# The rows of an MLP norm transposed by VectorE and placed by DMAs, in place of TensorE's transposes

## The chip, the cores and the metric

The kernel runs on one core of a Trainium2 chip. The metric is the time of one execution on the device, in microseconds (us). The core has five engines that run side by side, each with its own queue of instructions in a fixed order: TensorE (PE in the profile; its weight loads are PEld), VectorE (DVE), ScalarE (ACT), GpSimd (POOL) and SyncE (SP), which issues nearly all of this kernel's DMAs.

## The reference

Input rows `x` (4 batches, 1024 tokens, 512 features, float32) first pass a graph-attention layer, then a transformer block with six modulation vectors made from a condition. Only the last part of the block matters here, the MLP with its layer norm:

```python
x = x + g_msa * _attention(_modulate(_layernorm(x), sh_msa, sc_msa), W_qkv, W_out, b_out)
x = x + g_mlp * _ff(_modulate(_layernorm(x), sh_mlp, sc_mlp), W1, b1, W2, b2)

def _modulate(x, shift, scale):
    return x * (1.0 + scale) + shift
def _ff(x, W1, b1, W2, b2):
    return jax.nn.gelu(x @ W1 + b1, approximate=False) @ W2 + b2
```

The hidden width of the MLP is 2048. Everything is float32.

## The kernel before, in words

The 4096 rows are 32 tiles of 128 rows (`NTA`), and the MLP stage, the last of three, takes them in eight blocks of four tiles (`VB = 4`, the loop over `k` from L1603). The rows after attention lie in DRAM as `x2d[0..31]`.

For each block the normalised rows are needed with the features along the partitions: the tile `hT[1, 0]`, 128 partitions by 4 feature chunks by 512 rows. There is one such tile, and every block uses it. It is the moving operand of the up projection.

Both projections are done by a scheme with seven products in place of eight block products (`seven`, L520, and `with_four`, L564, which makes it seven steps: a, c, b, a2, b2, d, b3). A step is a group of matmuls into one PSUM bank and then some work on it by ScalarE or VectorE: after a, ScalarE copies the bank (L555); after c, `keep_c` copies it to SBUF on ScalarE (L544); after b, `start_d` on VectorE writes bank d (L547), which the product d adds to; after b2, `last` on VectorE reads bank b (L551), which the product b3 then adds to. The scheme needs sums of input pieces: `mlp_rows` (L630) makes them from `hT[1, 0]` on GpSimd with four operations (L512), into places 0 to 2 of the tile `tx["mlp"]`, the third of them in place in `hT`. The first is needed by product c, the second by b, the third by b2, the last by b3. Places 3 and 4 of the same tile hold the gate and the bias of the current batch, spread over all partitions; place 5 is not used.

One block `k` goes so:

- `norm_load(1, k + 1)` loads the four row tiles of the next block from `x2d` into `xl` (four buffers, L412).
- The up projection: four groups `p`, each with seven steps into the banks `up_banks` ("mau" to "mdu" in the profile), a Gelu on ScalarE (L661) and four sums on VectorE (`up_sums`, L504 to L507). In group 2, `norm_rows` normalises the next block's rows in place on VectorE (L425).
- The down projection: seven steps into `dn_banks` ("mad" to "mdd"). After each step's matmuls `dn_done` (L1653) multiplies by the gate and adds to the row tiles `rows2` on VectorE (L1656, L1661), and the finished halves are stored on SP (L1664).
- After the first step of the down projection `between()` (L1637) is called, once a block. It transposes the next block's rows with `norm_T` (L433): for each of the four feature chunks, four TensorE transposes (L443) into a bank of the up projection (`new_bank`, L1592, alternates between two), then one operation that applies scale and shift and writes `hT[1, 0]`, on ScalarE (L448) or VectorE (L450), in turn; in block 0 all four on ScalarE. Then it loads gate and bias for a new batch (every second block), loads the block's rows once more as `rows2` (they take the four `xl` buffers, so each load waits until the transposes have read them), makes the sums by `mlp_rows`, and adds the bias to each `rows2` on GpSimd (L1651).

In block 0 VectorE also makes sums of the weights `w2` just before the down projection (L1626). The rows of the very first block are transposed earlier, inside the attention stage, by the same `norm_T`.

No planner orders this stage: every engine's instructions stand in the order in which this code emits them. An engine whose next instruction waits holds all that stands behind it. A tile's buffers are handed on by waiting for the last reader.

Two older places do on other data what the change will do here: in the attention stage `turn` (L1184) transposes 32x32 blocks on VectorE and moves them by DMAs from SBUF to SBUF (`wT<-wd`, L1195); and at the start `spread_values` (L363) moves many pieces of 128 bytes (`vb<-vrd`).

Of the kernel before, what the change touches and what calls it, by code (L numbers as in the profile page):

```python
# [12 lines left out]
F32 = mybir.dt.float32  # L13
I32 = mybir.dt.int32
AF = mybir.ActivationFunctionType
ALU = mybir.AluOpType
# [3 lines left out]
P = 128  # L20
S = 1024
F = 512
FC = F // P
NT = S // P
# [17 lines left out]
def cond_block_kernel(  # L42
# [27 lines left out]
    nc = tc.nc  # L70
# [27 lines left out]
    modT = cst.tile([P, 4 * FC, B], F32, name="modT")  # L98
    SH_A, SC_A, SH_M, SC_M = 0, FC, 2 * FC, 3 * FC
# [20 lines left out]
    def spread(k, b, o):  # L120

        nc.sync.dma_start(o, gated[32 * k + b : 32 * k + b + 1, :].broadcast_to([P, F]))
# [6 lines left out]
    x2d = [tc.dram_tile([P, F], F32, name=f"x2d{i}") for i in range(NTA)]  # L129


    with ExitStack() as gctx:
# [272 lines left out]
        rp = ctx.enter_context(tc.tile_pool(name="rp", bufs=1, side="right", reuse_waits="tile"))  # L405
        qp = ctx.enter_context(tc.tile_pool(name="qp", bufs=1, side="right", reuse_waits="tile"))
        xp = ctx.enter_context(tc.tile_pool(name="xp", bufs=1, side="right", reuse_waits="tile"))
        VB = 4
        xl, hT, wqk, wv, qT, kT, w1g, part = {}, {}, {}, {}, {}, {}, {}, {}
# [23 lines left out]
        def norm_T(st, k, c, bank, on_act=True):  # L433

            sh, sc = NORM[st][4:]
            b = k * VB // NT
            if st == 1 and k > 0:
                hT[st, k] = hT[st, 0]
            elif c == 0:
                hT[st, k] = rp.tile([P, FC, VB * P], F32, name="hT", tag="hT", bufs=2)  # L440
            pt = bank("ptn")
            for n in range(VB):
                nc.tensor.transpose(  # L443
                    pt[:, n * P : (n + 1) * P], xl[st, k * VB + n][:, c * P : (c + 1) * P], ident
                )
            scale, shift = modT[:, sc + c, b : b + 1], modT[:, sh + c, b : b + 1]
            if on_act:
                nc.scalar.activation(hT[st, k][:, c, :], pt, AF.Identity, scale=scale, bias=shift)  # L448
            else:
                nc.vector.tensor_scalar(hT[st, k][:, c, :], pt, scale, shift, ALU.mult, ALU.add)  # L450

        def load_w(held, key, tag, src, cols):

# [136 lines left out]
        ex, tx = {}, {}  # L590
# [350 lines left out]
    with ExitStack() as actx:  # L941
# [298 lines left out]
        for b in range(B):  # L1240
# [22 lines left out]
            for gp in range(NP):  # L1263
                g, p = divmod(gp, 2)
# [284 lines left out]
    with ExitStack() as mctx:  # L1549
        mp = mctx.enter_context(tc.tile_pool(name="mp", bufs=1, reuse_waits="tile"))  # L1550
        hs[2] = mp.tile([P, NT, HB], F32, name="hs2")
        hs[3] = mp.tile([P, NT, HB], F32, name="hs3")
        for i in (6, 7):
            put_w1(i, mp.tile([P, FC, 2, P], F32, name=f"w1_{i}"))
        for i in range(4, MC // 2):
            mlp_weights(nc.vector, i, lambda: mp.tile([P, 3 * HB], F32, name="ex", tag="ex", bufs=4))
        emit(NS + 4, NS + 24)
        octx.close()
        pctx.close()
        mp2 = mctx.enter_context(tc.tile_pool(name="mp2", bufs=1, reuse_waits="tile"))  # L1560
        ps = mctx.enter_context(tc.tile_pool(name="ps3", bufs=1, space=PSUM))
        w2s = [mp2.tile([P, 4, F], F32, name=f"w2_{k}") for k in range(4)]
        for k in (0, 2, 1, 3):
            nc.sync.dma_start(w2s[k], w2[k * F : (k + 1) * F, :].rearrange("(c p) f -> p c f", p=P))
        w2x = [mp2.tile([P, 3, 4, HB], F32, name=f"w2x{k}") for k in range(2)]
        for p in range(4):
            hx[p] = mp2.tile([P, 3, 2, HB], F32, name=f"hx{p}")
        up_banks, dn_banks = (
            {n: ps.tile([P, F], F32, name=n + x) for n in ("ma", "mb", "mc", "md")} for x in "ud"
        )  # L1570
        for banks in (up_banks, dn_banks):
            for n in ("mb", "md"):
                nc.tensor.matmul(banks[n], lhsT=ident, rhs=hT[1, 0][:, 0, :], start=True, stop=True)
        gate2, bias2 = (tx["mlp"][:, k, :] for k in (3, 4))

        def dn_lhs(which, t, c):
            p, q = divmod(c, 2)
            rows = slice(t * P, (t + 1) * P)
            at = {4: 0, 5: 1, 2: 2}.get(which)
            if at is not None:  # L1580
                return hx[p][:, at, q, rows]
            return hs[p][:, 2 * {0: 0, 1: 1, 6: 2, 3: 3}[which] + q, rows]

        def dn_rhs(which, t, c):
            k, r = divmod(c, 4)
            at = {4: 0, 5: 1, 3: 2}.get(which)
            if at is not None:
                return w2x[k][:, at, r, :]
            h, f = {0: (0, 0), 1: (1, 0), 2: (1, 1), 6: (0, 1)}[which]
            return w2s[2 * h + k][:, r, f * HB : (f + 1) * HB]  # L1590

        def new_bank(name):  # L1592

            flip.append(0)
            return up_banks[("ma", "mc")[len(flip) % 2]]

        def short():
            return mp2.tile([P, F], F32, name="s", tag="s", bufs=2)

        flip = []  # L1600
        rows2 = {}
        NB2 = NTA // VB
        for k in range(NB2):  # L1603
            b = k * VB // NT
            nxt = k + 1
            if nxt < NB2:
                norm_load(1, nxt)
            for p in range(2 if k == 0 else 0, 4):
                steps = with_four(
                    get=up_banks.get, short=short, lhs=up_lhs(p), rhs=up_rhs, nk=2,  # L1610
                    room=lambda: hidden(p, 1, 1), done=lambda i, j, t: gelu(p, i, j, t),
                )
                for n, f in enumerate(steps):
                    f()
                    if k == 0 and n == (4 if p == 2 else 2):

                        for j in ((0, 1) if p == 2 else (2,)):
                            up_sums(j)
                if k > 0:
                    up_sums(p)  # L1620
                elif p == 3:
                    sums = []
                    for j in range(2):
                        o = [w2x[j][:, n] for n in range(3)]
                        q, r = w2s[j], w2s[2 + j]
                        sums.append(steps_b(nc.vector, o, q[:, :, :HB], q[:, :, HB:], r[:, :, :HB], r[:, :, HB:]))  # L1626
                    for n, two in enumerate(zip(*sums)):
                        for f in two:
                            f()
                        if n == 0:  # L1630
                            up_sums(p)
                if p == 1 and k == 1:
                    rstd(rs2, mv2, nm2, 3 * NT, NTA)
                if p == 2 and nxt < NB2:
                    norm_rows(1, nxt)

            def between():  # L1637
                if nxt < NB2:
                    for c in range(FC):
                        norm_T(1, nxt, c, new_bank, on_act=(k == 0 or c % 2 == 1))  # L1640
                if k * VB % NT == 0:
                    spread(2, b, gate2)
                    spread(3, b, bias2)
                for n in range(VB):
                    i = k * VB + n
                    rows2[n] = rp.tile([P, F], F32, name="x2", tag="xl", bufs=VB)
                    nc.sync.dma_start(rows2[n], x2d[i])
                if nxt < NB2:
                    mlp_rows()
                for n in range(VB):  # L1650
                    nc.gpsimd.tensor_tensor(rows2[n], rows2[n], bias2, ALU.add)  # L1651

            def dn_done(i, j, t):  # L1653
                y = t if (i, j) == (1, 1) else short()
                g = gate2[:, j * HB : (j + 1) * HB].unsqueeze(1).to_broadcast([P, 2, HB])
                nc.vector.tensor_tensor(  # L1656
                    y.rearrange("p (t f) -> p t f", t=2), t.rearrange("p (t f) -> p t f", t=2), g, ALU.mult
                )
                for n in range(2):
                    o = rows2[2 * i + n][:, j * HB : (j + 1) * HB]  # L1660
                    nc.vector.tensor_tensor(o, o, y[:, n * HB : (n + 1) * HB], ALU.add)  # L1661
                    if (i, j) in ((0, 1), (1, 0)):
                        at = k * VB + 2 * i + n
                        nc.sync.dma_start(out[at * P : (at + 1) * P, :], rows2[2 * i + n])  # L1664

            steps = with_four(
                get=dn_banks.get, short=short, lhs=dn_lhs, rhs=dn_rhs, nk=MC // 2, room=None, done=dn_done
            )
            for n, f in enumerate(steps):
                f()  # L1670
                if n == 0:
                    between()


# [48 lines left out]
```

## Time and profile before

| | us |
|---|---|
| median of three runs | 3037.48 |
| lowest and highest of the three | 3035.5 and 3040.55 |
| span of the profiled execution, first to last instruction | 3034.2 |
| TensorE busy in it | 2999.3 (99%) |
| VectorE, ScalarE, GpSimd busy | 1999.6, 1432.0, 1339.4 |
| the MLP's up and down products, from 2262 us on | 772 of the span |
| one block of the MLP stage, start to start | 99.2 |

No time of its own is given for the profiled execution besides its span; the span lies 3.3 us under the median of the three runs and 1.3 us under the lowest.

How the profile is read: "busy" is the time in which an engine worked on something. The forty slices are equal parts of the span (76 us each), and each digit is the busy share in tenths. The chain of waits starts at the last instruction and goes back from each step to what released it. In a row of instructions, `hT<-mcu,modT` means that `hT` is written from `mcu` and `modT`; then come the shapes, the count after x, the busy time and the mean in ns. Rows marked SPq are DMA instructions on SP's queue: their times are those of issuing, not of moving the bytes.

### The profile page before, as it was taken

The page shows a single profiled execution, that of the slowest core. Times are in us where ns is not written, and L with a number is a line of the kernel's source. Part 1 is how long each engine was busy: PE and PEld are TensorE (multiplying, and loading weights), DVE is VectorE, ACT ScalarE, POOL GpSimd, SP SyncE. Part 2 cuts the span into 40 slices and gives each one's busy share as a digit, 9 for nine tenths or more (in the row PEclk, how much of TensorE's full clock was granted, in tenths as well). Part 3 has the DMA queues.
Part 4 walks back from the last instruction along what each step waited for, and adds up shares of the span by engine and source line. Part 5 has one row for each costly group of instructions (what it writes and reads, how often), then busy time and mean ns, then how long its engine had stood idle before and what let it go on. Part 6 is the DMA issues. An engine that isn't in the chain of part 4 may idle for free.

```text
span 3034.2 us, 41780 instructions
## 1 busy us (share of the span) xinstructions
PE 2999.3 (99%) x15317; PEld 1980.2 (65%) x15317; DVE 1999.6 (66%) x2836; ACT 1432.0 (47%) x2368; POOL 1339.4 (44%) x922
## 2 busy tenths in 40 slices
PE   9999999999999999999999999999999999999999
PEld 6666655555555555555555555555568888888888
DVE  3888867777878877878787878877863222222322
ACT  3344456555755565755555755556641221112211
POOL 1444456555656655656655656655721110111010
PEclk9999999999999999999999999999999999999999
DMA  6433357777868777768777868766871010101110
GB/s 201 140 118 121 117 129 180 162 171 179 192 157 210 181 168 179 192 155 211 187 159 180 191 159 205 189 162 164 203 196 63 14 49 28 49 21 35 35 42 15
DMA packets 282695, 417.90 MB, mean 138 GB/s; under 512 B 28968, under 2 KB 101092, under 8 KB 282492
## 3 DMA queue, kind: packets, MB, share of 16 engines
q1 hardware_dynamic: 282256, 415.03, 53.8%
q8 instruction: 123, 2.02, 0.3%
q14 instruction: 80, 0.66, 0.1%
q10 hardware_dynamic: 236, 0.20, 0.0%
HBM read 120.93 MB, written 25.76 MB: 48 GB/s over the span
## 4 chain that ended last, share of the span: by engine, by line
PE 83%; DVE 7%; ACT 3%; POOL 3%; issue 2%; DMA 2%; SPq 1%; POOLq 0%; DVEq 0%; ACTq 0%
PE q L533 19%; PE psc L1156 15%; PE pav L1064 13%; PE pu L1139 6%; PE mbd L533 5%; PE mbu L533 5%; PE mad L533 4%; PE mau L533 3%; PE mcd L533 2%; PE mdd L533 2%; PE mdu L533 2%; PE mcu L533 2%; DVE mx L1167 1%; ACT w L1173 1%; POOL t L742 1%
## 5 line engine op out<-in xcount | busy, mean ns | idle before, releaser
L1182 POOL TENSOR_SCALAR w<-w,sm 128x1024 f32<-128x1024 f32 x256 | 728.6, 2846 | 701.5 <-DVE sm L1178 686.4
L1173 ACT ACTIVATE w<-psc,mx 128x1024 f32<-128x1024 f32 x512 | 570.7, 1115 | 642.6 <-DVE mx L1167 641.6
L1191 DVE STREAM_TRANSPOSE wd<-w 128x1024 f32<-128x1024 f32 x512 | 632.2, 1235 | 109.3 <-ACT w L1180 96.0
L1167 DVE TENSOR_REDUCE mx<-psc 128x1 f32<-128x1024 f32 x512 | 599.2, 1211 | 80.2 <-PE psc L1156 77.0
L1156 PE MATMUL psc<-kT,qT 64*128 64x512 f32 x2048 | 526.9, 615 | 3.1 <-ACT kT L1024 1.4
L1064 PE MATMUL pav<-wT,v 128*64 128x256 f32 x4096 | 482.1, 383 | 1.2 <-DMA wT<-wd 0.6
L1064 PEld LDWEIGHTS pav<-wT,v 128*64 128x64 f32 x4096 | 296.1, 137 | 224.0 <-issue 86.0
L1156 PEld LDWEIGHTS psc<-kT,qT 64*128 64x128 f32 x2048 | 201.6, 186 | 220.5 <-issue 151.2
L1180 ACT ACTIVATE w<-w,sm 128x1024 f32<-128x1024 f32 x256 | 291.0, 1137 | 0.0
L512 POOL TENSOR_TENSOR tx<-hT 128x512 f32<-128x512 f32 x8 | 10.3, 1288 | 596.5 <-ACT hT L448 596.5
L1148 DVE TENSOR_TENSOR xr<-pu,xr 128x512 f32<-128x512 f32 x210 | 143.5, 683 | 78.9 <-PE pu L1139 78.7
L533 PE MATMUL q<-hT,wqk 128*128 128x512 f32 (+1 forms) x396 | 181.2, 581 | 1.0 <-DVE q L547 1.0
L555 ACT COPY mbu<-mau 128x512 f32<-128x512 f32 x30 | 17.1, 570 | 276.5 <-PE mau L533 276.5
L719 PE MATMUL pa<-kp,sfT 128*128 128x320 f32 x512 | 143.5, 433 | 1.4 <-ACT sfT L694 1.4
L533 PEld LDWEIGHTS q<-hT,wqk 128*128 128x128 f32 x396 | 74.7, 190 | 80.9 <-issue 78.2
L533 PE MATMUL q<-tx,ex 128*128 128x512 f32 (+1 forms) x264 | 123.5, 591 | 1.8 <-POOL tx L618 1.3
L719 PEld LDWEIGHTS pa<-kp,sfT 128*128 128x128 f32 x512 | 94.8, 190 | 38.2 <-ACT sfT L694 1.9
L679 PE MATMUL pf<-wx,xT 128*128 128x512 f32 x256 | 116.0, 596 | 0.0
L533 PE MATMUL mad<-w,hs 128*128 128x256 f32 x512 | 113.1, 379 | 0.0
L533 PEld LDWEIGHTS mad<-w,hs 128*128 128x128 f32 x512 | 97.3, 190 | 13.2
L1139 PE MATMUL pu<-wout,oT 128*128 128x256 f32 x360 | 98.4, 396 | 4.2 <-DVE xr L1148 3.7
L1139 PEld LDWEIGHTS pu<-wout,oT 128*128 128x128 f32 x360 | 62.6, 189 | 59.3 <-issue 31.6
(309 smaller groups left out, 4590.7 us busy)
## 6 DMA issues: line engine op xcount, KB each, us to landing
wT<-wd SPq DMA_DIRECT2D x1024, 256.0 KB
wqk<-in_w_qkv SPq DMA_DIRECT2D x64, 256.0 KB
xT<-in_xt SPq DMA_DIRECT2D x32, 256.0 KB
xs<-in_x SPq DMA_DIRECT2D x32, 256.0 KB
x1d<-xs SPq DMA_DIRECT2D x32, 256.0 KB
xl<-x1d SPq DMA_DIRECT2D x32, 256.0 KB
wv<-in_w_qkv SPq DMA_DIRECT2D x32, 256.0 KB
xr<-x1d SPq DMA_DIRECT2D x32, 256.0 KB
```

What stands on the lines that cost most here:

```text
L533: nc.tensor.matmul(t[:, q * width : (q + 1) * width], lhsT=lhs(which, q, k), rhs=rhs(which, q, k), start=(fresh and q == 0 and k == 0), st ...
L679: nc.tensor.matmul(pfs[i], lhsT=xT[i][:, c, :], rhs=wx[:, c, :], start=False, stop=(c == FC - 1), skip_group_check=True,)
L719: nc.tensor.matmul(pas[i][:, n, :HF], lhsT=sfT2[i][:, c, :], rhs=kp[:, b, c, n * HF : (n + 1) * HF], start=False, stop=(c == FC - 1), skip ...
L1064: nc.tensor.matmul(po[j * D : (j + 1) * D, :], lhsT=vt[b, g][:, m, p * P + j * D : p * P + (j + 1) * D], rhs=w[:, j, :, m, :], start=(m == 0),
L1139: nc.tensor.matmul(pu[0][:, q * HB : (q + 1) * HB], lhsT=a[:, q * P : (q + 1) * P], rhs=r, start=(bool(fresh) and q == 0), stop=True, skip ...
L1148: nc.vector.tensor_tensor(o, pu[0].rearrange("p (r f) -> p r f", r=2), o, ALU.add)
L1156: nc.tensor.matmul(sc[j][:, n * F : (n + 1) * F], lhsT=qT[b, gp][q, t * P : (t + 1) * P], rhs=kT[b, gp][q, n * F : (n + 1) * F], start=Tru ...
L1167: nc.vector.tensor_reduce(mx, sc, axis=AX.X, op=ALU.max, negate=True)
L1173: nc.scalar.activation(w, sc, AF.Exp, bias=mx, accum_out=sm)
L1180: nc.scalar.mul(w, w, sm)
L1182: nc.gpsimd.tensor_scalar(w, w, sm, None, ALU.mult)
L1191: nc.vector.transpose(wd[j][:, :, at, :], wn.pop((b, gp, t, j)).rearrange("p (m k) -> p m k", k=U))
```

## The change

For the MLP stage's second to eighth block the transposes leave TensorE. `norm_turn` transposes one tile of 128 rows on VectorE: one instruction that transposes each 32x32 block where it lies, from `xl` into place 5 of `tx["mlp"]`. What is then still in the wrong place is moved by sixteen DMAs: one for each pair of a group `u` of 32 rows (now a group of 32 partitions) and a group `v` of 32 features. Each moves 32 partitions by four feature chunks by 32 values, 16 KB in pieces of 128 bytes, into `hT[1, 0]`. All are issued by SP. `norm_mod` then applies scale and shift in place in `hT[1, 0]` on ScalarE, one instruction for each feature chunk.

`between` is now called after each of the seven steps of the down projection. After each of the first four steps it turns one of the next block's tiles, loads one tile of `rows2` and adds its bias; after the first also gate and bias where the batch is new. After the fifth it calls `norm_mod` four times and `mlp_rows`. All four tiles of a block use the same place 5, so the next tile's transpose waits until the sixteen DMAs of the one before have read it. `new_bank` goes. The first block's rows are still transposed by TensorE in the attention stage.

```diff
@@ norm_T
-            if st == 1 and k > 0:
-                hT[st, k] = hT[st, 0]
-            elif c == 0:
+            if c == 0:
                 hT[st, k] = rp.tile([P, FC, VB * P], F32, name="hT", tag="hT", bufs=2)
...
+        RB = 32
+
+        def norm_turn(i, t):
+
+            xl_i = xl.pop((1, i))
+            nc.vector.transpose(
+                t.rearrange("p (m k) -> p m k", k=RB), xl_i.rearrange("p (m k) -> p m k", k=RB)
+            )
+            blocks = t.rearrange("p (c v r) -> p c v r", c=FC, r=RB)
+            for u in range(P // RB):
+                at = i % VB * P + u * RB
+                for v in range(P // RB):
+                    nc.sync.dma_start(
+                        hT[1, 0][RB * v : RB * (v + 1), :, at : at + RB], blocks[RB * u : RB * (u + 1), :, v, :]
+                    )
+
+        def norm_mod(k, c):
+
+            b = k * VB // NT
+            o = hT[1, 0][:, c, :]
+            scale, shift = modT[:, SC_M + c, b : b + 1], modT[:, SH_M + c, b : b + 1]
+            nc.scalar.activation(o, o, AF.Identity, scale=scale, bias=shift)
...
-            def between():
-                if nxt < NB2:
+            def between(n):
+                if n < VB:
+                    if nxt < NB2:
+                        norm_turn(nxt * VB + n, tx["mlp"][:, 5, :])
+                    if n == 0 and k * VB % NT == 0:
+                        spread(2, b, gate2)
+                        spread(3, b, bias2)
+                    rows2[n] = rp.tile([P, F], F32, name="x2", tag="xl", bufs=VB)
+                    nc.sync.dma_start(rows2[n], x2d[k * VB + n])
+                    nc.gpsimd.tensor_tensor(rows2[n], rows2[n], bias2, ALU.add)
+                if n == VB and nxt < NB2:
                     for c in range(FC):
-                        norm_T(1, nxt, c, new_bank, on_act=(k == 0 or c % 2 == 1))
-                if k * VB % NT == 0:
-                    spread(2, b, gate2)
-                    spread(3, b, bias2)
-                for n in range(VB):
-                    i = k * VB + n
-                    rows2[n] = rp.tile([P, F], F32, name="x2", tag="xl", bufs=VB)
-                    nc.sync.dma_start(rows2[n], x2d[i])
-                if nxt < NB2:
+                        norm_mod(nxt, c)
                     mlp_rows()
-                for n in range(VB):
-                    nc.gpsimd.tensor_tensor(rows2[n], rows2[n], bias2, ALU.add)
...
             for n, f in enumerate(steps):
                 f()
-                if n == 0:
-                    between()
+                between(n)
```

More of the change, by code (lines that the diff above doesn't have):

```diff
@@ L1590, in dn_rhs @@
             return w2s[2 * h + k][:, r, f * HB : (f + 1) * HB]
-        def new_bank(name):
-            flip.append(0)
-            return up_banks[("ma", "mc")[len(flip) % 2]]
         def short():
             return mp2.tile([P, F], F32, name="s", tag="s", bufs=2)
-        flip = []
         rows2 = {}
```

## The prediction

> **What bounds the kernel now.** I read the page first, then the chain of waits over one block of the MLP stage, then the timeline around the transposes there, then the rows of DMA issue. The page:
>
> ```profile
> span 3034.2 us, 41780 instructions
> PE 2999.3 (99%) x15317; PEld 1980.2 (65%) x15317; DVE 1999.6 (66%) x2836; ACT 1432.0 (47%) x2368; POOL 1339.4 (44%) x922
> ...
> DVE  3888867777878877878787878877863222222322
> ACT  3344456555755565755555755556641221112211
> POOL 1444456555656655656655656655721110111010
> ...
> DMA  6433357777868777768777868766871010101110
> ```
>
> TensorE is busy for 99% of the span, so only TensorE time, or a new wait of TensorE, moves the end. From slice 31 on (the MLP stage, 2262 us to the end) the other engines and the DMAs are at 0 to 3 tenths: there is room for work moved off TensorE. The chain of waits for one block (start, us, what):
>
> ```profile
> 2683.40 6.91 PE mad L533 x32
> 2690.30 0.45 PE mcu L443 x4
> 2690.75 0.03 issue
> 2690.78 0.82 DVE hT L450
> 2691.60 0.04 issue
> 2691.64 0.66 PE mcu L443 x4
> 2692.30 0.46 PE mau L443 x4
> 2692.76 6.91 PE mcd L533 x32
> ```
>
> The down projection's second product starts 2.46 us after its first ends (2692.76 against 2690.31). Those 2.46 us are the four groups of transposes and one wait for a PSUM bank that VectorE is emptying.
>
> **What it removes.** Steady blocks: 2.46 us on the chain, six times. Block 0: 2.67 us (2293.46 to 2296.13, where ScalarE empties all four banks). The other mcd starts agree to 0.01 us, and the last block, which has no next block, shows no gap. Sum 6 x 2.46 + 2.67 = 17.4 us. The 12 evictions on VectorE (0.81) and 16 on ScalarE (0.78) go too; beyond the wait counted above they were off the chain.
>
> **What it adds.** 28 transposes on VectorE, 448 DMAs of 16 KB on SP's queue, 28 in-place scalings on ScalarE. Nothing of it is on TensorE; it costs time only if it is late. So I work out when each arrives, with T = 0 at the start of the block's down projection, whose seven products take 6.91 us each (the rows above) and which ends at T+48.4. The prices:
>
> ```profile
> L1191 DVE STREAM_TRANSPOSE wd<-w x512: 1203/1235/1248, 415.2 to 2232.9; 128x1024 f32<-128x1024 f32 x171
> L1191 DVEq EVENT_SEMAPHORE  x506: 21/50/508, 431.7 to 2227.4; - x169
> ...
> 42.85 6.66 SPq L363 DMA_DIRECT2D vb<-vrd  x18
> ...
> 422.35 1.30 SPq L1195 DMA_DIRECT2D wT<-wd  x2
> ...
> 34.56 0.32 SPq L311 DMA_DIRECT2D qrd<-qrows  x1
> 36.63 0.33 SPq L313 DMA_DIRECT2D qrB<-qrd  x1
> ```
>
> A transpose of half the width: 1.235 / 2 = 0.62 us. There is one staging tile, so the next transpose waits for all sixteen landings: at 50 ns a wait 0.8 us at most, I take 0.4. Landing: the second DMA of qrd, which needs the first, is issued 2.07 us after it, so some 1.7 us remain after the last issue slot. The issue price i is not shown for this transfer, and decides. Low end: vb, 0.37 to 0.39 us each (18 in 6.66, 18 in 7.02), pieces of 128 bytes in a three-dimensional pattern of equal shape on both sides, as the new DMAs have, but read from DRAM. High end: wT, 0.65 each (two in 1.30 with the DMAs idle before), at its shortest 0.54 + 0.04 between = 0.58; it is the only transfer from on-chip memory to on-chip memory, but reshapes 32 rows into 128 and moves 256 KB. I take 0.39: piece size, pattern and size are vb's. The DMA engines are no limit: vb's 80 pieces took a DMA share of 0.10 to 0.20 while being issued. Nor does such traffic slow the products: mcd took 6.91 us with the DMAs at 0.9 share (2694 to 2697), as the idle ones did.
>
> One tile's cycle is 0.62 + 0.4 + 1.7 + 16 i = 2.7 + 16 i, with i = 0.39: 8.9 us.
>
> Steady block. VectorE is free of up_sums at T+2.2 (2685.19 against 2683.02). Transposes start at 2.2 and 11.1; the third stands behind start_d, which waits for the third product (20.7) and ends at 21.5; the fourth at 30.4. Behind the fourth on VectorE stands last, which must free bank b for the seventh product: done at 31.8, due at 41.4. The fourth tile lands at 39.3. ScalarE scales at 0.75 us a row (0.805 on its own in norm_row, a little less back to back): the first two by 40.8, all by 42.3; the next block's first product is due at 48.4. GpSimd is later: rows2[3] is loaded behind the sixteen DMAs on SP (issued 37.3, some 3.1 us with 1 us for its 256 KB, so 40.4), its bias add (1.27) ends at 41.7, and mlp_rows stands behind that: first sum 42.9, due when product c starts at 50.1. All covered with 7 us to spare.
>
> Block 0. VectorE does the w2 sums first and is free at T+9.4 (2295.77 against 2286.38). Transposes at 9.4, 18.3, 27.2, 36.1; last done at 37.5 (due 41.4); the fourth tile lands at 45.0, two rows scaled at 46.5 (due 48.4), first sum at 48.6 (due 50.1). Covered, with 1.5 us to spare. What is late next there is the first sum.
>
> The moved rows2[0] and rows2[1]: issued by 18.3, landed by 21.4, bias added by 22.7, due on VectorE at 27.7 (end of a2).
>
> SP has nothing else queued before the out stores (first at T+45, before the last products' rows only), apart from the rows2 loads named and every second block's two spreads (0.45 each), due with the first bias add. So the added work costs 0, and 3034.2 - 17.4 = 3016.8 us of span. The page's span stands 3.3 us under the median of the three times (3037.48); with that added I predict 3020 us.
>
> **A rule that speaks against it.** The rows above let eighteen small DMAs follow each other at 0.37 us while each lands 2 us later, so landings overlap. The Trainium skill, "DMA: Bandwidth & Descriptors", section "Rules for kernel authors", asks to merge many small transfers and says that under 64 KB one pays mostly overhead; "Anatomy of one DMA" there gives 2.0 us of fixed cost for each (GpSimd's path). Taken one after the other that would be 32 us a tile and an estimated 80 us late per block, over 500 us in all; the 18 in 6.66 us say that it is not taken so.
>
> **Rivals.**
> (1) Issue at wT's price. At i = 0.58 the cycle is 12.0. Steady: fourth transpose at 38.2, landed 50.2, first row scaled 51.0 against 48.4, and the first sum another 1.1 late behind rows2[3]: 3.7 us a block. Block 0: landed at 57.4, 58.2 against 48.4, so 9.8 + 1.1. Sum 6 x 3.7 + 10.9 = 33, net 3053. At i = 0.65 (13.1): steady 8.1, block 0 15.3, sum 64, net 3084. Here the fourth transpose holds last past 41.4 as well. For: the one on-chip to on-chip row. Against: its unequal shapes, and its size. Over the seven blocks the sum is 28 x cycle - 303.3 (24 of the 28 from the steady ones); it passes the 17.4 at a cycle of 11.45, i = 0.547, and from there the change is slower than before.
> (2) Only block 0 pays: i between 0.42 and 0.5 (the spreads and 128-row loads stand at 0.45 in a row). At 0.45 the cycle is 9.9, block 0 is 2.6 us late, 3022.6; at 0.5 5.8 us, 3026. For: block 0's 1.5 us of slack. Against: vb's two rows.
> (3) Late landing. If a landing takes 2 us more than 2.07 (the 1.7 becomes 3.7), at i = 0.39 the cycle is 10.9: steady 0, block 0 6.6 us, 3027. Nothing in these stretches is that slow; wT's bytes, with idle DMAs, moved within 1.65 us of the issue at 422.35 (DMA share 0.00 up to 423, 0.30 up to 424).
> (4) i between 0.5 and 0.58, around break-even: 3026 to 3053.
>
> **How the numbers follow.** Forecast (i up to 0.42) 0.44; (2) and (3) 0.13; (4) 0.10; (1) 0.33. A measurement of this kernel can't tell changes under about 0.2% (6 us) from none. Faster by more, under 3031.4: the forecast, (2), (3), and a little of (4): 0.58. Within, to 3043.5: 0.06 of (4). Slower: the rest, 0.36. Low end 3016: the whole gain and the spread of the three times. High end 3066: it leaves the upper part of (1) out, some 0.19. The forecast's own range is 3016 to 3026.
>
> **What would show it.** Right: no gap between the first two products of a down projection and none before the next block's first; the new DMAs at 0.37 to 0.42 us each, sixteen within one product; VectorE's third transpose straight after start_d, not after a landing. Wrong: sixteen DMAs taking 9 us or more; TensorE waiting at a block's start for ScalarE's scaling (on landings) or at product c for GpSimd; the seventh product waiting for last. Time lost in block 0 alone is (2). What would make it wrong is above all i past 0.5.

## The result, and the profile after

| | us |
|---|---|
| before, median of four runs (lowest, highest) | 3039.02 (3035.5, 3046.95) |
| after, median of four runs (lowest, highest) | 3085.01 (3084.18, 3090.21) |
| ratio after / before, 95% interval | 1.0149 [1.0131, 1.0168] |
| the profiled execution after: time, span | 3085.75, 3084.0 |

The change costs 1.5%: the spans are 49.8 us apart (3084.0 - 3034.2). It was forecast to gain 17. Rival (1), "issue at wT's price", had 3084.

The page of the changed kernel:

```profile
span 3084.0 us, 42214 instructions
PE 3008.1 (98%) x15205; PEld 1976.7 (64%) x15205; DVE 2031.6 (66%) x2852; ACT 1439.7 (47%) x2380; POOL 1344.2 (44%) x922
...
DVE  4888867777878877878777878878853223223322
...
DMA  6433357767778777778776878766841211211120
...
PE 68%; SPq 10%; DVE 8%; DMA 4%; issue 3%; POOL 3%; ACT 3%; DVEq 0%; POOLq 0%; ACTq 0%
PE q L554 18%; PE psc L1177 14%; PE pav L1085 13%; SPq L462 8%; PE pu L1160 5%; PE mbu L554 4%; PE mau L554 4%; PE mcu L554 2%; DMA hT<-tx 2%; PE mdu L554 2%; SPq L1216 1%; DVE mx L1188 1%; POOL t L763 1%; ACT w L1194 1%; DMA wT<-wd 1%
```

In the MLP stage, the last nine slices, VectorE and the DMAs are nearly as empty as before. The last two lines are the chain that ended last: SP's issuing of the new DMAs (`SPq L462`) stands in it with 8% of the span, some 250 us, and their landing (`DMA hT<-tx`) with 2%. Work meant to lie beside the products has become the path.

One line has their price (min/median/max in ns):

```profile
L462 SPq DMA_DIRECT2D hT<-tx x448: 585/599/1893, 2298.3 to 2975.8; - x150
```

0.60 us, and 0.04 us to the next. Sixteen take 10.24 us at best, 10.55 on average and 11.72 at most, where one of them is held up.

The timeline of one block, whose down projection starts at T = 2609.78 (start, us, what; the idle time before it in brackets):

```profile
2609.78 7.07 PE L554 MATMUL mad<-w,hs 128*128 128x256 f32 x32
...
2611.67 0.70 DVE L455 STREAM_TRANSPOSE tx<-xl 128x512 f32<-128x512 f32 x1
2612.46 11.24 SPq L462 DMA_DIRECT2D hT<-tx  x16
2616.69 7.07 PE L554 MATMUL mcd<-w2x,hx 128*128 128x256 f32 x32
...
2625.36 0.71 DVE L455 STREAM_TRANSPOSE tx<-xl 128x512 f32<-128x512 f32 x1 [12.99 <-DMA hT<-tx]
2626.10 10.24 SPq L462 DMA_DIRECT2D hT<-tx  x16
...
2637.89 0.71 DVE L455 STREAM_TRANSPOSE tx<-xl 128x512 f32<-128x512 f32 x1 [6.42 <-DMA hT<-tx]
...
2651.10 0.71 DVE L455 STREAM_TRANSPOSE tx<-xl 128x512 f32<-128x512 f32 x1 [9.81 <-DMA hT<-tx]
2651.74 0.65 DVE L572 TENSOR_TENSOR s<-mbd,s 128x512 f32<-128x512 f32 x1
2651.84 10.24 SPq L462 DMA_DIRECT2D hT<-tx  x16
...
2652.45 7.17 PE L554 MATMUL mbd<-w2x,hs 128*128 128x256 f32 x32 [1.06 <-DVE s L572]
...
2662.13 0.59 SPq L1660 DMA_DIRECT2D x<-x2d  x1
2663.44 2.93 ACT L471 ACTIVATE hT<-hT,modT 128x512 f32<-128x512 f32 x4 [39.06 <-DMA hT<-tx]
2664.31 3.78 PE L554 MATMUL mau<-hT,wqk 128*128 128x256 f32 x8 [4.68 <-ACT hT L471]
2664.98 1.27 POOL L1661 TENSOR_TENSOR x<-x,tx 128x512 f32<-128x512 f32 x1 [10.73 <-DMA x<-x2d]
2666.20 1.26 POOL L533 TENSOR_TENSOR tx<-hT 128x512 f32<-128x512 f32 x1
...
2667.88 3.05 PE L554 MATMUL mcu<-tx,ex 128*128 128x256 f32 x8
```

What was to go did go: `mcd` follows `mad` after 6.91 us. But the four transposes are 13.7, 12.5 and 13.2 us apart (each waits for `DMA hT<-tx`), the last sixteen DMAs are issued by 2662.08, the rows are scaled from 2663.44, and TensorE stands from 2659.63 to 2664.31. The seventh product waits 1.06 us for `last`, which stands behind the fourth transpose. And GpSimd's first sum (L533, over at T+57.7) stands behind the bias add of the fourth row tile, whose load stands on SP behind the sixteen DMAs: product c (`mcu`), which could have started at T+50.1, starts at T+58.1, once the first product, slow itself at 3.78 us, is done as well.

The account, from the starts of the `mad` products: without any wait a block takes 96.69 us (measured in the kernels below), before it took 99.16, 99.38 for block 0. Going to 96.69 removes 17.5 us in seven blocks. After, block 0 takes 111.01 and the six others 103.61 to 105.88: 14.3 and together 50.5 us over 96.69. 64.8 - 17.5 = 47.3; the other 2.5 us lie outside the seven blocks (the stage's first `mad` 1.8 us later, the end 0.6).

### The profile page after: what moved, and what is told of

It reads as the page before. It is cut to its first block, busy times and chain, and to the rows that moved or that the text cites. A ratio compares the mean times of both kernels' runs of the same rounds, so it can differ in the third digit from the quotient of the medians.

```text
span 3084.0 us, 42214 instructions
## 1 busy us (share of the span) xinstructions
PE 3008.1 (98%) x15205; PEld 1976.7 (64%) x15205; DVE 2031.6 (66%) x2852; ACT 1439.7 (47%) x2380; POOL 1344.2 (44%) x922
## 4 chain that ended last, share of the span: by engine, by line
PE 68%; SPq 10%; DVE 8%; DMA 4%; issue 3%; POOL 3%; ACT 3%; DVEq 0%; POOLq 0%; ACTq 0%
PE q L554 18%; PE psc L1177 14%; PE pav L1085 13%; SPq L462 8%; PE pu L1160 5%; PE mbu L554 4%; PE mau L554 4%; PE mcu L554 2%; DMA hT<-tx 2%; PE mdu L554 2%; SPq L1216 1%; DVE mx L1188 1%; POOL t L763 1%; ACT w L1194 1%; DMA wT<-wd 1%
## 5 line engine op out<-in xcount | busy, mean ns | idle before, releaser
L1661 POOL TENSOR_TENSOR x<-x,tx 128x512 f32<-128x512 f32 x32 | 43.0, 1346 | 680.3 <-DMA x<-x2d 649.0
L455 DVE STREAM_TRANSPOSE tx<-xl 128x512 f32<-128x512 f32 x28 | 19.9, 709 | 200.0 <-DMA hT<-tx 200.0
L471 ACT ACTIVATE hT<-hT,modT 128x512 f32<-128x512 f32 x28 | 20.5, 802 | 277.3 <-DMA hT<-tx 277.3
L1675 DVE TENSOR_TENSOR x<-x,s 128x256 f32<-128x256 f32 x64 | 47.3, 764 | 96.7 <-POOL x L1661 95.1
L554 PEld LDWEIGHTS mad<-w,hs 128*128 128x128 f32 x512 | 97.3, 190 | 13.2
```

Of the source, the lines that this page charges most:

```text
L554: nc.tensor.matmul(t[:, q * width : (q + 1) * width], lhsT=lhs(which, q, k), rhs=rhs(which, q, k), start=(fresh and q == 0 and k == 0), st ...
```

## The experiments

The theory after the result: the price of issuing one of these DMAs, 0.64 us where 0.39 was taken, times sixteen, in series with a transpose and a landing for each tile, makes the cycle outrun the down projection. Three questions: what makes the price; whether the price or the wait for the one staging place costs the time; and what part the slow first products at the block's start have (3.78 and 3.05 us where a product of that size took 1.73).

**What makes the price.** Each tile's sixteen DMAs in four kinds:

```diff
-                    nc.sync.dma_start(hT[1, 0][cols, :, at : at + RB], blocks[rows, :, v, :])
+                    if u == 0:
+                        nc.sync.dma_start(hT[1, 0][cols, :, at : at + RB], blocks[rows, :, v, :])
+                    if u == 1:
+                        far = x2d[i].rearrange("p (c v r) -> p c v r", c=FC, r=RB)
+                        nc.sync.dma_start(hT[1, 0][cols, :, at : at + RB], far[rows, :, v, :])
+                    if u == 2:
+                        nc.sync.dma_start(dump[cols, :], t[rows, v * P : (v + 1) * P])
+                    if u == 3:
+                        far = dumpd.rearrange("p (c v r) -> p c v r", c=FC, r=RB)
+                        nc.sync.dma_start(far[rows, :, v, :], blocks[rows, :, v, :])
```

> The sixteen DMAs of a tile are split into four kinds of four, all 16 KB and 128-byte pieces, in this order: (1) as in the change; (2) the same pattern, read from x in DRAM instead of the staging tile; (3) on chip to on chip, but flat, 32 rows of 512 bytes, into a tile nobody reads; (4) the pattern of the change from the staging tile to a DRAM tile nobody reads. Three quarters of the next block's rows are so not placed; that part of the computation is left out. Theory (both ends on chip make the price): kinds 1 and 3 at 0.64 us each, kinds 2 and 4 at 0.35 to 0.42; sixteen take some 8.2 us, a cycle of 11, the time 3018 to 3035. Rival (small pieces and the three-dimensional pattern make it): 1, 2 and 4 at 0.64, only 3 at about 0.4; sixteen take 9.3 us, a cycle of 12.1, about 3055. Rival (any DMA issued in such a row, as the x loads at 0.59 between them): all four at 0.6 or more, 3085.

The four kinds in the order of the diff:

```profile
L464 SPq DMA_DIRECT2D hT<-tx x112: 593/602/784, 2297.0 to 2974.1; - x112
L467 SPq DMA_DIRECT2D hT<-x2d x112: 596/597/1572, 2299.7 to 2976.7; - x112
L469 SPq DMA_DIRECT2D dump<-tx x112: 570/589/1567, 2302.3 to 2979.2; - x112
L472 SPq DMA_DIRECT2D dumpd<-tx x112: 548/598/1687, 2304.8 to 2982.4; - x112
```

All four at 0.59 to 0.60; the one run took 3092.8 us. My first account, that both ends on chip make the price, was wrong, and so was small pieces: kind 3 moves whole rows of 512 bytes. It fits the third rival, but `vb`'s 0.37 was still unexplained. One thing set my DRAM kinds apart from `vb`: a row of `x2d` is as long as its pitch, so 32 rows by 4 chunks fall together into one dimension of 128 there, and the two sides' patterns differ. `vb`'s sides are equal, dimension for dimension.

One more reading: here the first product of a block was hardly late (its DMAs into `hT` come first, the other kinds last), yet blocks still took 105.5 to 106.8 us, as product c waited some 6 us for GpSimd. GpSimd's sum, behind the last x row, is what ends last.

**The same with equal patterns.** The DRAM sides get a row pitch longer than the row, and kind 3 is now read from DRAM. Kind 4 differs from the run before in the pitch alone:

```diff
-                        far = x2d[i].rearrange("p (c v r) -> p c v r", c=FC, r=RB)
+                        far = w1[:P, :F].rearrange("p (c v r) -> p c v r", c=FC, r=RB)
...
-                        nc.sync.dma_start(dump[cols, :], t[rows, v * P : (v + 1) * P])
+                        nc.sync.dma_start(dump[cols, :], w1[rows, v * P : (v + 1) * P])
...
-                        far = dumpd.rearrange("p (c v r) -> p c v r", c=FC, r=RB)
+                        far = dumpd[:, :F].rearrange("p (c v r) -> p c v r", c=FC, r=RB)
```

> The run that mixed four kinds had all four at 0.60 us, with the DRAM kinds' rows merged into one long dimension on the DRAM side, so that the two sides' patterns differed. Here the DRAM side has a row pitch longer than the row, so both sides keep the same pattern. Four DMAs of each kind a tile: (1) as in the change, on chip to on chip; (2) 32 x 4 pieces of 128 bytes from DRAM (rows of w1) to the same places; (3) 32 rows of 512 bytes from DRAM to a tile nobody reads; (4) 32 x 4 pieces of 128 bytes from the staging tile to a DRAM tile nobody reads. The placing of three quarters of the next block's rows is left out. Theory (a DMA costs 0.64 a slot unless one side is DRAM and both sides have the same pattern, as vb's has): kind 1 at 0.64, kinds 2 to 4 at 0.37 to 0.45; sixteen take 7 to 8 us, the cycle is 9.7 to 10.7, below break-even, TensorE waits nowhere, 3018 to 3026. Rival (any DMA that shares the row with on-chip ones, or stands in this stage, pays 0.64): all four at 0.6, 3085 to 3093. Rival (DRAM helps only in one direction): kind 4 or kind 2 at 0.6.

```profile
L464 SPq DMA_DIRECT2D hT<-tx x112: 591/599/937, 2298.5 to 2915.9; - x112
L467 SPq DMA_DIRECT2D hT<-in_w x112: 351/430/1337, 2301.1 to 2918.1; - x112
L469 SPq DMA_DIRECT2D dump<-in_w x112: 374/420/1663, 2303.3 to 2920.0; - x112
L472 SPq DMA_DIRECT2D dumpd<-tx x112: 302/430/550, 2305.1 to 2921.9; - x112
```

As the theory had it: 0.60 against 0.42 to 0.43. So here a DMA is issued at the low price when one side is in DRAM and both sides have the same pattern, and at the high one when either fails, whichever of the two. Both failing seems to cost no more: `wT` took 0.54 at its shortest and 0.66 and 0.60 with the DMAs idle before, though 0.97 in the median among its busy DMAs. What in the queue makes the difference, the runs do not show. The mean distance between a block's transposes fell from 12.92 us to 10.83, below the prediction's break-even of 11.45, and its one run, in which three quarters of the rows are not placed, took 3031.3 us: five of the seven blocks ran at 96.69, block 0 took 105.97 and the next 97.54. My 3018 to 3026 missed block 0, which is the prediction's rival (2) at work.

**Half of the DMAs from ScalarE's queue.**

```diff
-                    nc.sync.dma_start(
+                    (nc.sync, nc.scalar)[u // 2].dma_start(
```

> Eight of a tile's sixteen DMAs are issued from ScalarE's queue instead of SP's. Theory (the issue price of one queue makes the cycle): 8 x 0.644 + 0.71 + 0.1 + 1.9 = 7.9 us a tile instead of 13, TensorE waits nowhere, 3017 to 3026. Rival (the price is that of something both queues share, or of the DMA engines): each DMA takes some 1.2 us on either queue, the cycle stays at 13, 3080 to 3090. Rival (the wait for the landings of the single staging place): the cycle falls by less than the 5 us of issue.

3021.37 us, ratio 0.9945 [0.993, 0.996]. The timeline of the third and fourth tile, and the next block's start:

```profile
2602.36 0.71 DVE L455 STREAM_TRANSPOSE tx<-xl 128x512 f32<-128x512 f32 x1 [0.44 <-DMA hT<-tx]
2603.13 5.43 SPq L462 DMA_DIRECT2D hT<-tx  x8
...
2610.01 0.71 DVE L455 STREAM_TRANSPOSE tx<-xl 128x512 f32<-128x512 f32 x1 [0.40 <-DMA hT<-tx]
...
2619.24 2.93 ACT L471 ACTIVATE hT<-hT,modT 128x512 f32<-128x512 f32 x4 [24.41 <-DMA x<-x2d]
2620.89 1.37 POOL L533 TENSOR_TENSOR tx<-hT 128x512 f32<-128x512 f32 x1 [0.23 <-ACT hT L471]
...
2628.57 1.89 PE L554 MATMUL mau<-hT,wqk 128*128 128x256 f32 x8
2630.30 1.89 PE L554 MATMUL mcu<-tx,ex 128*128 128x256 f32 x8
```

Each queue keeps its price (SP 0.600, ScalarE 0.612), so nothing that both share sets it. The cycle is 7.5 to 9 us, except at the first tile (12.0 to 14.3): ScalarE's first eight DMAs stand behind its copy of bank a, which waits for the first product. Scaling starts at T+39, 9 us early (T = 2580.23), and every block takes 96.69 us. The whole gain is there.

The Trainium skill ("DMA: Bandwidth & Descriptors", "Issuing engines are not separate DMA queues") says that issuing from several engines saves only the sequencer's time, "which is usually small relative to the DMA itself". What it says of the kind of saving holds here, of its size not: that time was 10.5 of a cycle of 12.9 us, and halving it took the kernel from 3085.0 to 3021.4 us.

**No staging place.** The four tiles are transposed in place, in the up projection before, and all 64 DMAs are issued from T on, SP alone:

```diff
                 if p == 2 and nxt < NB2:
                     norm_rows(1, nxt)
+                    for i in range(VB):
+                        norm_turn(nxt * VB + i)
...
+                if n == 0:
+                    for i in range(VB + 1):
+                        if i < VB and nxt < NB2:
+                            norm_place(nxt * VB + i)
+                        if i > 0:
+                            rows2[i - 1] = rp.tile([P, F], F32, name="x2", tag="xl", bufs=VB)
+                            nc.sync.dma_start(rows2[i - 1], x2d[k * VB + i - 1])
+                            nc.gpsimd.tensor_tensor(rows2[i - 1], rows2[i - 1], bias2, ALU.add)
```

> The four tiles are transposed in place during the up projection before; all 64 DMAs of a block are issued from SP one after another from the start of the down projection, with no transpose and no landing between them; each x row load follows the DMAs of the tile behind it. Theory (issue alone): 64 x 0.644 + 3 x 0.5 = 42.7, landed at T+44.7, so TensorE's first product is not late; the fourth x row comes at 48, VectorE and GpSimd stand late behind it by 0 to 5 us a block: 3018 to 3045, between the change and its full gain. Rival (the wait on the single staging place is the cost, the issue price would hide): the whole gain, no row late, DMAs at 0.4. Rival (64 DMAs in flight slow each other): over 0.7 us each, 3060 or more.

3026.54 us, ratio 0.9961 [0.9946, 0.9975]. The price stays, and TensorE's only new wait in the stage is in block 0, behind transposes that now delay VectorE in its up projection:

```profile
L463 SPq DMA_DIRECT2D hT<-xl x448: 585/599/1701, 2286.1 to 2913.9; - x150
...
PE mbu L555 <- DVE mdu L569: 2.7, 1, 2.7
```

Behind that wait the clock is at half for 3.41 us, and the next two products take 3.02 and 2.59 us in place of some 1.9. Steady blocks take 96.73. So the same 448 DMAs at the same price are hidden when they are alone (64 x 0.644 = 41 us; 43.5 to 44.9 with the x row loads between them, against 48.4). Neither the price nor the wait on the staging place is the cost by itself: it is their sum, four times 10.5 + 2.4 us, that passes the down projection.

**One DMA for four tiles.** The four row tiles lie in one tile of `hT`'s layout; one DMA moves a pair (u, v) for all of them, 64 KB:

```diff
+        def norm_turn():
+            t = xl4[1].rearrange("p c (m k) -> p (c m) k", k=RB)
+            nc.vector.transpose(t, t)
+        def norm_place():
+            src, dst = (a.rearrange("p c (n k) -> p (c n) k", k=P) for a in (xl4[1], hT[1, 0]))
+            for u in range(P // RB):
+                for v in range(P // RB):
+                    nc.sync.dma_start(
+                        dst[RB * v : RB * (v + 1), :, RB * u : RB * (u + 1)],
+                        src[RB * u : RB * (u + 1), :, RB * v : RB * (v + 1)],
+                    )
```

> The four tiles lie side by side in one tile of the layout of the block's transposed rows, are transposed in place by one instruction of 128x2048 in the up projection before (2.8 us by the rate of the half-width ones), and one DMA moves what four moved: 16 DMAs of 64 KB a block instead of 64 of 16 KB, with the same pieces of 128 bytes. Theory (a price per DMA): 16 x 0.644 = 10.3 us, landed by T+14 to T+18, nothing late, all 17.4 us kept: 3018 to 3024. Rival (a price per piece, or the bytes): 2.6 us each, 41 us, landed at T+43, the x rows behind them later than VectorE wants them: 3030 to 3085.

3025.28 us, ratio 0.9958 [0.9941, 0.9974]:

```profile
L476 SPq DMA_DIRECT2D hT<-xl x112: 586/632/1608, 2290.4 to 2880.8; - x112
...
PE mbu L569 <- DVE mdu L583: 3.6, 1, 3.6
```

Four times the pieces and bytes cost 0.63 us instead of 0.60: nearly all of the price is for each DMA. The one wait left is again in block 0's up projection, behind the transpose. Moving that to the start of the down projection:

```diff
                 if p == 2 and nxt < NB2:
                     norm_rows(1, nxt)
-                    norm_turn()
...
                     if nxt < NB2:
+                        norm_turn()
                         norm_place()
```

> As the kernel with one DMA for four tiles, but the one transpose of 128x2048 stands at the start of the down projection, ahead of the DMAs, instead of in the up projection before, where block 0's TensorE waited 3.6 us behind it. Theory (that wait is the place of the transpose alone): the 3.6 us go, DMAs from T+5 in steady blocks and T+12 in block 0, landed by T+25 at the latest, nothing late, 3019 to 3023. Rival (the DMAs' start matters, VectorE or GpSimd are late behind the x rows): 3025 or more.

3020.69 us, ratio 0.9943 [0.9928, 0.9958], with every block at 96.69:

```profile
2580.81 2.30 DVE L469 STREAM_TRANSPOSE xl<-xl 128x2048 f32<-128x2048 f32 x1
2583.20 11.82 SPq L476 DMA_DIRECT2D hT<-xl  x16
...
2596.80 2.93 ACT L486 ACTIVATE hT<-hT,modT 128x512 f32<-128x512 f32 x4 [3.28 <-DMA hT<-xl]
```

With T = 2578.92 the rows are scaled by T+21. 0.6 us of the wait in block 0 stay. The two-queue version, this one and the two between them beat both kernels; this one and the two-queue version gain most, 16 to 18 us on the one before.

**The slow first products.** The clock that TensorE was granted, in the block shown above (the stretch; PE, PEld, DVE, ACT, POOL busy; then PEclk, DMA share, GB/s):

```profile
2662.00:2664.00 2.00, 0.00 (x0) 0.00 (x0) 0.00 (x0) 0.56 (x1) 0.00 (x0) 0.85 0.40 106
2664.00:2666.00 2.00, 1.69 (x4) 1.37 (x5) 0.00 (x0) 2.00 (x4) 1.02 (x1) 0.50 0.11 42
...
2670.00:2672.00 2.00, 2.00 (x10) 1.77 (x9) 1.97 (x4) 0.58 (x1) 1.69 (x2) 0.95 0.62 234
```

After TensorE's idle time its clock is at half. The test fills the idle time with products nobody reads:

```diff
             for n, f in enumerate(steps):
                 f()
                 between(n)
+            if nxt < NB2:
+                for r in range(7):
+                    nc.tensor.matmul(up_banks["ma"], lhsT=ident, rhs=w2s[0][:, r % 4, :], start=True, stop=True)
```

> The change, with seven products of the identity with a slab of w2 (128x512, 0.43 us each, results not read) put between a block's last product and the next block's first, where TensorE waits 4.7 to 5.2 us for the scaled rows. Theory (TensorE's clock is granted at half for some 6 us because it idled): the first two products of the next block, 3.78 and 3.05 us, fall to 1.73 each; the rows land no earlier, so 3.1 to 3.4 us are saved in each of six blocks and perhaps a little in block 0: 3062 to 3068. Rival (those products are slow because they wait for the scaling row by row or share memory with it): unchanged, 3083 to 3088.

3081.58 us. Each filler was two matmuls of 0.43 us, so the seven took 6.0 us, not 3:

```profile
2656.33 6.17 PE L1688 MATMUL mau<-w,ident 128*128 128x512 f32 x14
2662.34 1.89 PE L554 MATMUL mau<-hT,wqk 128*128 128x256 f32 x8
2664.07 1.96 PE L554 MATMUL mcu<-tx,ex 128*128 128x256 f32 x8
```

The products ran at full clock, but the time hardly moved (ratio to before 1.0146 [1.0129, 1.0163]); it lies between the two forecasts and meets neither. The same with four fillers, `range(4)`:

> As the run with seven filler products, with four, 3.4 us instead of 6.0, so that the fillers end before the scaled rows land (idle 4.7 to 5.2 us) and leave TensorE 1.3 to 1.8 us without work. With seven, the first products ran at full clock, yet only 0.8 us a block was saved, as the fillers were up to 1.1 us too long and product c then waited for GpSimd's first sum, which ends at T+56 to T+57.8. Theory (the half clock comes from the long idle, but GpSimd's sum stands right behind it): both products at 1.73 us, product c starts when the sum is there, about T+57.2 against 50.1 due, so a block takes 96.7 + 7.1 = 103.8 us instead of 105.1: 3074 to 3079. Rival (an idle of 1.3 us already halves the clock): the products at 3 to 3.8 us and 3083 to 3087. Rival (the half clock alone is what holds the block up, GpSimd is not): 3062 to 3068.

3085.62 us, ratio 1.0164 [1.0147, 1.0181]: nothing gained, above my range. The time is that of the second rival, but not its sign: the products were slow in one block of six. One block (`mad` at 2611.52), TensorE and then GpSimd:

```profile
2660.58 3.60 PE L1688 MATMUL mau<-w,ident 128*128 128x512 f32 x8
2665.44 2.27 PE L554 MATMUL mau<-hT,wqk 128*128 128x256 f32 x8 [1.26 <-ACT hT L471]
2668.70 1.99 PE L554 MATMUL mcu<-tx,ex 128*128 128x256 f32 x8 [0.99 <-POOL tx L533]
```

```profile
2667.39 1.26 POOL L533 TENSOR_TENSOR tx<-hT 128x512 f32<-128x512 f32 x1
```

At full clock the first product is done early and product c then stands until GpSimd's first sum ends (2668.65): the time goes back into a wait. The six steady blocks of this profile took 104.71 us on average against 105.10 (104.27 with seven fillers), and the stages before happened to be 2.2 us longer in it. GpSimd's sum ended 0.3 us later on average, and one block still fell to half clock. So the half clock is real, but most of the 3 us by which the two products are slow is hidden behind GpSimd: by these profiles 0.4 to 0.8 us a block were got back. That is small beside the spread of single blocks (103.07 to 105.88), and the times of four runs show no gain clear of it. The third rival, the half clock alone, falls.

## Why the prediction was wrong

- **The 17.4 us removed: right.** `mcd` follows `mad` at once, and a gapless block is 2.47 us shorter than a steady one before, 17.5 us in all.
- **The issue price: here it fell.** "I take 0.39: piece size, pattern and size are vb's." It is 0.644 with what lies between, the high end of my two rows. I had put the two rows apart by likeness of shape; what counted was that `vb` has one side in DRAM *and* equal patterns, and the new DMAs only the second. With two rows 1.7 times apart, the right reading was that sixteen times the difference, 4 us a tile, decides the sign, and that the row of the same kind of memory on both sides (`wT`) was the warning.
- **The other terms of the cycle: a little high.** Transpose 0.71 us instead of 0.62 (half the width is not half the time); landing and waits together less than taken: what is not issue is 2.4 us of the mean cycle of 12.92 (10.55 of issue, the slower DMAs included), where 2.7 was taken. The cycle came to 12.9, not 8.9. One reading in rival (3) was wrong: `wT`'s bytes had not moved within 1.65 us. Up to 424 the trace before has 43 GB/s for 1 us, some 43 KB of the 256; no sum rested on it.
- **When each part is late: right, with the other price.** Rival (1) at 13.1 had the steady block 8.1 us late (the first sum behind the fourth x row included), block 0 15.3, `last` held up, 64 us, 3084. Measured: 50.5 / 6 = 8.4, 14.3, the seventh product waiting 0.7 to 1.1 us in four of the six and 7.2 in block 0, 64.8, 3085.0. Inside the 8.4, GpSimd's sum is 7.2 late (it ends at T+57.3 on average, due T+50.1), as the cycle is shorter than 13.1; the other 1.2 come from the half clock, which I had not foreseen. So it is partly luck that 3084 was met so closely: at the measured cycle the same sum gives 28 x 12.92 - 303.3 = 58.5 us, and the half clock made up the rest.
- **Break-even at a cycle of 11.45: held up, as far as one run can say.** At 10.83 it was faster than before, and mostly block 0 paid: 9.3 us, where the prediction's working for that cycle gives 6.2.
- **"The DMA engines are no limit": right.** The DMA share was 0.15 to 0.19 while the new DMAs of the block shown were issued, 0.54 with 64 KB each, and the price was nearly the same with 16 KB and 64 KB.
- **The rule on small transfers: it pointed the right way by another mechanism.** The Trainium skill's advice to merge transfers under 64 KB ("DMA: Bandwidth & Descriptors", "Rules for kernel authors") I had set aside because landings overlap. They do, but the issue slots do not: merging four into one took the issue from some 42 us a block (four times 10.55) to 10.8 to 12.2 and turned the loss into the gain.

## What to carry to other kernels

Price a DMA by its issue slot on its queue, times the count, and take the slot from a row with the same kinds of memory at both ends and patterns related in the same way; likeness of piece size said nothing here. When a chain of issue, landing and one staging place must fit under a product, any one of three cures did it here: split the queue, remove the staging wait, or merge the DMAs. When a wait ends, look at what ended just behind it: the half clock looked like 3 us a block, and filling the idle time got back 0.8 at most, because another engine was nearly as late.

## What the runs showed of the hardware that was not expected

- Two issue prices on SP: 0.42 to 0.43 us back to back with one side in DRAM and equal patterns (0.34 for `vb`), 0.59 to 0.63 otherwise. The loads of `xl` show it too: mostly 0.32 to 0.41 as whole rows, 0.58 to 0.63 where the same 256 KB go into a split layout. A low-price DMA straight behind a high-price one takes 0.59 as well (the x row loads behind the sixteen; in the second price run 0.588 for the first of kind 2, 0.430 for the next three).
- Half clock after idling, from the trace's clock record: 3.41, 6.83 or 10.24 us long, so in steps of 3.41. Idle times of 4.3 us and more brought it each time, in all runs. Shorter ones brought it sometimes: 1.32 us (two queues, in the attention stage), 1.93 (block 0 after), 2.05 and 2.23 (four fillers) and 2.72 (no staging place) did, but 2.09 (four fillers), 3.57 (one DMA for four tiles) and all others of 1.3 to 1.8 did not. In each run all changes of the clock lie whole steps of 3.41 us apart (2327.89 us, or 682 steps, from the record's start to the first in the changed kernel); that where in a step the idle time falls decides would fit, but was not tested. Two blocks with the same lateness of GpSimd (T+56.5 and T+56.6) and half clocks of 3.41 and 6.83 us took 103.61 and 105.10. The Trainium skill ("TensorE: Matmul & The Clock Gate", "HAM oscillation — how this bites in real kernels") warns of idle gaps above some 3.4 us. The step length agrees with that figure, the limit does not: here 1.32 us was enough once, and 3.57 us was not.
- VectorE's adds of 128x256 from two SBUF tiles took 0.42 us alone. In the changed kernel 35 of 64 lay beside a GpSimd operation: 16 of them took 1.47 to 1.54 us, 14 took 0.77 and 5 still 0.42; before the change none lay beside one. The Trainium skill ("SBUF — State Buffer", "Who interferes with whom") says that a VectorE instruction with two SBUF inputs contends with a GpSimd instruction that reads SBUF, and calls the port pair that they share "an exclusive lock"; up to 1.1 us more, beside GpSimd operations of 1.26 to 1.49 us, agrees with it.
- A VectorE transpose of 512, 1024 and 2048 columns took 0.71, 1.24 and 2.30 us: some 0.18 fixed and 0.53 for each 512 (worked out from the first and last).
